# Score products in steps with three double steps per block, and attention blocks of 496 columns, in a two-layer graph kernel

## The chip, the core and the metric

The kernel runs on one core of a Trainium2 chip. The metric is the device time of one launch in microseconds (us). The engines are TensorE (PE; its weight loads are PEld), VectorE (DVE), ScalarE (ACT), GpSimd (POOL) and SyncE (SP, which only issues DMAs here). Every engine works through its own queue in order and waits on semaphores for the others.

## What is computed

Two layers on a graph with 3327 nodes and 128 features. The first is one graph convolution with batch norm; it takes under 3% of the time. The second is an attention over the reshaped features: 128 "batches" d, each with 3327 x 3327 scores of rank 8, to which the adjacency matrix is added twice.

```python
# layer 1, on h = relu(layernorm(x)); n = 3327, d = 128, 8 features per score
q = (x @ Wq.T).reshape(d, n, h)
k = (x @ Wk.T).reshape(d, n, h)
v = (x @ Wv.T).reshape(d, n, h)
a = jnp.einsum('dnh,dmh->dnm', q, k) * scale
a = a + spatial_encoding + edge_encoding      # both are adj
a = jax.nn.softmax(a, axis=2)
out = jnp.einsum('dnm,dmh->dnh', a, v)
return out.reshape(n, h * d) @ Wo.T
```

All is in float32. The scores never go to memory: exp of them is taken on the chip, and numerator and denominator of the softmax come from one product with v and a column of ones.

## The kernel before

**Tiling.** The 128 batches are taken in 32 groups of four. A group goes through seven blocks of columns n (`blocks`, L68: six of 512 and one of 255), and a block through 13 steps. The 3327 rows m lie in 26 chunks c of 128 partitions; a chunk with four batches makes two *pairs* (c, half), each of two batches. So a block has 52 pairs, and a step four of them. `pairs(s)` (L682) says which.

**Two ways for a pair.** A *plain* pair takes its score from PE (`product`, L718, line L725, two matmuls into a PSUM tile of two banks), adds the adjacency on DVE (L818, `scalar_tensor_tensor`, into a third of a tile d), and later ACT takes exp of the whole tile d at once (L856, called `late`, after the first exp of the next step). A *weighted* pair goes past DVE: ACT takes exp of the score straight from PSUM (L828, tile f), and POOL multiplies it by exp of the adjacency terms (L831), which was computed once and lies in DRAM (`wd`). Before, the first 19 chunks are plain (WC = 19): 38 plain and 14 weighted pairs per block. Steps 0 to 11 have three plain pairs and one weighted, step 12 has two of each. A step with two weighted pairs is called a double step below.

**Order in a step.** The order is written by hand (`manual_schedule`), and each engine's queue follows it: score of the weighted pair and its exp; exp of the d of the step before; score and add of plain pair 0; first half of the products with v of the step three before (`second(0)`, L604, eight matmuls; LAG = 3); plain pair 1; plain pair 2, or the second weighted pair; what lies beside (`beside`, L756); the other half of the products with v (`second(1)`). Three PSUM tiles (`psc`) hold scores, two banks (`avs2`) hold the sums over m, there are four tiles d and five tiles f. A sum is ended by `finish` (L609) in four parts, one per step: a copy on DVE (L612), four transposes on PE (L619), three DVE operations (L626 to L629), a DMA.

**Beside it.** Each group loads the q, k, v of the next (`loads`, L153, SP's queue, with 14 casts of k on POOL, L180). Projections for later groups and the last product of earlier ones are spread over the steps: `beside` issues a matmul in step 7 and 10, its evacuation in 8 and 11, and its DMA in 9 and 12. `fetch` (L703) loads adjacency and weights two steps ahead on SP's queue. In group 0 the weights of the blocks 3 to 6 are made on the way (`more_weights`, L734: a load, an exp on ACT, a write); those of the first three are made in the first layer (`weigh_early`, L439).

**The hand-over.** Between the layers, ACT's queue issues the 16 loads of q for group 0 (L580), then sorts part of k (L583), takes the roots of the second norm (L591), and a last exp of weights (L598); the pools of the attention lie where those of the first layer lay.

Of the kernel before, what the change touches and what calls it, by code (L numbers as in the profile page):

```python
# [9 lines left out]
F32 = mybir.dt.float32  # L10
# [8 lines left out]
N = 3327  # L19
D = 128  # L20
# [5 lines left out]
NB = 512  # L26
G = 4
# [4 lines left out]
WC = 19  # L32
CH = 4 * NP // D
NG = D // G
EARLY = 3
# [9 lines left out]
def tile_two_layer_gnn(  # L45
# [23 lines left out]

    const = ctx.enter_context(tc.tile_pool(name="const", bufs=1))  # L70
# [27 lines left out]
    nc.vector.memset(ones, 1.0)  # L98
    eps = const.tile([P, 1], F32, name="eps")
# [29 lines left out]
    def q_loads(q, p0, d):  # L129

        qs = qT[:, bass.ds(d * N, NP)].rearrange("(a h) n -> a h n", h=H)
        return [(q[p0 + i * H : p0 + (i + 1) * H].bitcast(F32), qs[i // 2]) for i in range(4)]
# [153 lines left out]
    with tc.tile_pool(name="l0", bufs=1) as l0, tc.tile_pool(  # L286
        name="l0adj", bufs=3
    ) as ap, tc.tile_pool(name="l0s", bufs=2) as sp, tc.tile_pool(
        name="l0p", bufs=1, space=PSUM
    ) as pp:  # L290
        xs = l0.tile([P, NC, D], F32, name="xs")
        A = l0.tile([P, NC, D], F32, name="A")
        B = l0.tile([P, NC, P], F32, name="B")
# [139 lines left out]
        for y, (n0, w) in enumerate(blocks[:EARLY]):  # L433
            a = ap.tile([P, 7 * NB], F32, name="a")
            a7 = a.rearrange("p (c n) -> p c n", c=7)
            nc.sync.dma_start(a7[:, :, :w], adjr[:, WC:, n0 : n0 + w])
            weights.append((a7, n0, w))

        def weigh_early():  # L439
            a7, n0, w = weights.pop(0)  # L440
            nc.scalar.activation(a7[:, :, :w], a7[:, :, :w], AF.Exp, bias=low, scale=2.0)
            nc.sync.dma_start(
                wd[:, :, n0 : n0 + w].rearrange("c p n -> p c n"), a7[:, :, :w]
            )
# [72 lines left out]
        def residual(i):  # L517
            pt, cs = turned(i, A, acc[i])
            nc.vector.tensor_add(xs[:, cs, :], xs[:, cs, :], pt)
            nc.sync.dma_start(  # L520
                xd.rearrange("(c p) d -> p c d", p=P)[:, cs, :], xs[:, cs, :]
            )
# [20 lines left out]
        ov0 = l0.tile([P, D, H + 1], F32, name="ov0")  # L543
        nc.gpsimd.memset(ov0, 1.0)

        def project_now(j, banks):
            todo = projections(sp, B2[:, j * CH : (j + 1) * CH], j, True, ov0, low_half[:CH, 1:2])
            for p, b in zip(todo, banks):
                drive(p, b)
            for p in todo:  # L550
                drive(p)
                drive(p)
# [23 lines left out]
        for i in range(4, NQ):  # L576
            relu(i)
        for b in range(G):
            for args in q_loads(q, 32 * b, b):
                nc.scalar.dma_start(*args)  # L580
        for x, c in enumerate(range(0, NC, 4)):
            n = min(4, NC - c)
            (nc.scalar.copy if x % 2 else nc.gpsimd.tensor_copy)(  # L583
                k[:, c : c + n, :],
                ks.bitcast(F32).rearrange("g (p c) -> g c p", c=NC)[:, c : c + n, :],
            )
# [8 lines left out]
        for i in range(1, NQ):  # L595
            columns(i, i % 2 == 0)
        keep_columns(0, NQ)
        weigh_early()  # L598


# [8 lines left out]
    def finish(rp, av, d0, n0, w):  # L609

        avs = rp.tile([P, NB], F32, name="avs")
        nc.vector.tensor_copy(avs[:, :w], av[:, :w])  # L612
        yield

        J = 4 if w == NB else 3
        R = w // J
        pt = av.rearrange("p (j q) -> p j q", j=4)
        for j in range(J):
            nc.tensor.transpose(  # L619
                pt[:R, j, :], avs[:, j : j + (R - 1) * J + 1 : J], ident  # L620
            )
        yield
        pv = pt.rearrange("p j (b h) -> p b j h", h=32)
        ri = rp.tile([P, G, 4], F32, name="ri")

        nc.vector.tensor_scalar(ri[:R, :, :J], pv[:R, :, :J, H], 1e-30, None, ALU.max)  # L626
        nc.vector.reciprocal(ri[:R, :, :J], ri[:R, :, :J])  # L627
        o = rp.tile([P, G, 4, H], F32, name="oq")
        nc.vector.tensor_tensor(  # L629
            o[:R, :, :J, :],  # L630
            pv[:R, :, :J, :H],
            ri[:R, :, :J].unsqueeze(3).to_broadcast([R, G, J, H]),
            ALU.mult,
        )
        yield
        nc.sync.dma_start(
            attb[bass.ds(d0, G), n0 : n0 + w, :].rearrange(
                "b (p j) h -> p b (j h)", j=J
            ),
            o[:R, :, :J, :].rearrange("p b j h -> p b (j h)"),  # L640
        )
# [4 lines left out]

    with tc.tile_pool(name="zero", bufs=1) as zp:
        z = zp.tile([P, H], F32, name="zeros")
        nc.gpsimd.memset(z, 0.0)
        nc.gpsimd.dma_start(att[T:, :], z)  # L650

    def attention():


        with tc.tile_pool(name="adj", bufs=4) as ap, tc.tile_pool(
            name="adw", bufs=3
        ) as wp, tc.tile_pool(name="exd", bufs=4) as ep, tc.tile_pool(
            name="exf", bufs=5
        ) as fp, tc.tile_pool(
            name="res", bufs=2  # L660
        ) as rp, tc.tile_pool(name="wk", bufs=2) as wk, tc.tile_pool(
            name="wk1", bufs=1
        ) as wk1, tc.tile_pool(name="psc", bufs=3, space=PSUM) as psc, tc.tile_pool(
# [7 lines left out]
            ov = wk1.tile([P, D, H + 1], F32, name="ov")  # L671
            nc.gpsimd.memset(ov, 1.0)
            if True:
                steps = [
                    (i, y, s)
                    for i in range(NG) for y in range(len(blocks)) for s in range(SU)
# [5 lines left out]
                def pairs(s):  # L682


                    last = s == SU - 1
                    plain = [(j // 2, j % 2) for j in range(3 * s, 3 * s + 3 - last)]
                    rest = [(WC + s // 2, 1 - s % 2)]
                    return plain, rest + ([(NC - 1, 0)] if last else [])
# [3 lines left out]
                for x, (i, y, s) in enumerate(steps):  # L692
                    n0, w = blocks[y]
                    for c, _ in pairs(s)[0]:
                        if (0, i, y, c // 2) not in have:
                            have[0, i, y, c // 2] = None
                            wanted.append((x, 0, i, y, c // 2))
                    c = pairs(s)[1][0][0]
                    if (1, i, y, c) not in have:
                        have[1, i, y, c] = None  # L700
                        wanted.append((x, 1, i, y, c))

                def fetch(x):  # L703
                    while wanted and wanted[0][0] <= x:
                        _, kind, i, y, c = wanted.pop(0)
                        n0, w = blocks[y]
# [11 lines left out]
                def product(i, y, c, half):  # L718
                    q, k, _ = sets[i % 2]
                    n0, w = blocks[y]  # L720
# [10 lines left out]
                waiting, ending, pending = [], [], []  # L731
                late = None

                def more_weights(i, y, s):  # L734

                    k, phase = s // 3, s % 3
                    if i or y + 1 >= len(blocks) or y + 1 < EARLY or k > 3:
                        return
                    n0, w = blocks[y + 1]
# [16 lines left out]
                def beside(i, y, s):  # L756


                    for j in [1, 2] if i == 0 else [i + 2] if i + 2 < NG else []:
                        if (y, s) != (0 if i else 3 * (j - 1), 3):  # L760
                            continue
# [3 lines left out]
                    if s in (8, 11) and extra:  # L765
                        drive(extra[0])
                    if s in (9, 12) and extra:
                        drive(extra.pop(0))
                    if s in (7, 10) and extra:
                        drive(extra[0], avs2[(i * len(blocks) + y + 1) % 2])  # L770
# [3 lines left out]
                extra = []  # L774

                def second(part):

                    (i, y, s), es = waiting[0]
                    n0, w = blocks[y]
                    av = avs2[(i * len(blocks) + y) % 2]  # L780
# [8 lines left out]
                    if part:  # L789
                        waiting.pop(0)  # L790
                        if s == SU - 1:
                            ending.append(finish(rp, av, at(i), n0, w))
# [5 lines left out]

                for x, (i, y, s) in enumerate(steps):
                    n0, w = blocks[y]  # L800
                    fetch(x + PRE)
                    k = x - i * SU * len(blocks) - FROM[i]
# [4 lines left out]
                    while pending and (total - len(pending)) * (SU * len(blocks) - FROM[i] - 4) <= k * total:  # L807
                        pending.pop(0)()
                    more_weights(i, y, s)
                    due = len(waiting) == LAG  # L810
# [14 lines left out]
                    def weighted(c, half):  # L825
                        f = fp.tile([P, 2, NB], F32, name="f")
                        p = product(i, y, c, half)
# [10 lines left out]
                    weighted(*rest[0])  # L838
# [3 lines left out]
                    if due:  # L842
                        second(0)
                    step()
                    add(1, product(i, y, *plain[1]))
                    if len(rest) > 1:
                        weighted(*rest[1])
                    else:
                        add(2, product(i, y, *plain[2]))
                    beside(i, y, s)  # L850
                    if due:
                        second(1)
# [6 lines left out]
                late()  # L859
                while waiting:  # L860
                    second(0)
                    step()
                    second(1)
# [7 lines left out]
    def attention_shifted():  # L871

        with tc.tile_pool(name="shq", bufs=1) as shp, tc.tile_pool(
# [11 lines left out]
            with tc.For_i(0, D, G) as d0:  # L885
# [8 lines left out]
                for y, (n0, w) in enumerate(blocks):  # L894
# [169 lines left out]
```

## Time and profile before

| | us |
|---|---|
| median of 3 runs | 10513.71 (10511.46 to 10516.91) |
| the profiled execution | 10527.91, of it the span of instructions 10526.1 |
| first exp of a weighted pair | 291.66 after the span's start |
| end of the last exp | 10504.8 |
| PE / DVE / ACT / POOL busy | 94% / 92% / 95% / 71% |
| DMA engines | 56.3% of the time of 16 engines on SP's and ACT's queue |

In the profile a row names line, engine, operation, output and inputs and the shape; then come the busy time, the mean duration of one in ns, the idle time before such instructions and what ended it. In a timeline a row is start, duration, instruction, and in brackets idle time before it and its releaser. Consecutive instructions overlap a little, so what one costs on a full engine is read from start to start. A matmul's end in the profile is modelled.

### The profile page before, as it was taken

What the parts mean: (1) busy time and instruction counts of PE and PEld (TensorE: products, weight loads), DVE (VectorE), ACT (ScalarE), POOL (GpSimd) and SP (SyncE); (2) the same over time, 40 slices, a digit from 0 to 9 for tenths busy, and PEclk for the clock granted to TensorE, in tenths of its full rate; (3) what the DMA queues carried; (4) which work ended last, traced back from release to release, by engine and by line L of the source; (5) the groups of instructions that cost most, each with busy time, mean ns of one, the idle gap of its engine ahead of it and who ended that gap; (6) DMA issues with size and microseconds to landing.
All of it is one profiled execution on the core that took longest, in us unless ns stands there. A gap on an engine that the chain in (4) does not pass through costs nothing. (4 is left out here: it accounts for less than half of the span.)

```text
span 10526.1 us, 186778 instructions
## 1 busy us (share of the span) xinstructions
PE 9922.7 (94%) x72399; PEld 2813.8 (27%) x72399; DVE 9714.9 (92%) x9949; ACT 9948.5 (95%) x6200; POOL 7497.1 (71%) x3868
## 2 busy tenths in 40 slices
PE   7889999999999999999999999999999999999999
PEld 3222222222222222222222222222222222222222
DVE  5789999999999999999999999999999999999998
ACT  4889999999999999999999999999999999999998
POOL 0667777777777777777777777777777777777776
PEclk8899999999999999999999999999999999999999
DMA  7655555555555555555555555555555555555554
GB/s 241 192 168 163 157 168 165 163 162 160 162 166 165 164 162 157 161 170 163 160 162 157 165 170 165 160 158 163 164 169 163 162 163 158 165 165 167 156 152 128
DMA packets 1115761, 1731.67 MB, mean 165 GB/s; under 512 B 198350, under 2 KB 441932, under 8 KB 1107180
## 3 DMA queue, kind: packets, MB, share of 16 engines
q1 hardware_dynamic: 1110478, 1713.99, 56.3%
q8 instruction: 568, 9.31, 0.4%
q10 hardware_dynamic: 4350, 5.64, 0.2%
q14 instruction: 333, 2.73, 0.1%
q0 software_dynamic: 32, 0.00, 0.0%
HBM read 1618.76 MB, written 100.53 MB: 163 GB/s over the span
## 5 line engine op out<-in xcount | busy, mean ns | idle before, releaser
L818 DVE SCALAR_TENSOR_TENSOR d<-at,s 128x1024 f32<-128x1024 f32 x8512 | 9204.3, 1138 | 642.7 <-PE s L725 406.2
L831 POOL TENSOR_TENSOR f<-f,wt 128x1024 f32<-128x1024 f32 (+1 forms) x3136 | 6983.8, 2235 | 2619.1 <-ACT f L828 2572.0
L856 ACT ACTIVATE d<-d 128x3072 f32<-128x3072 f32 (+1 forms) x2912 | 7372.9, 2532 | 73.4 <-DVE d L818 70.5
L604 PE MATMUL av<-d,v 128*9 128x512 f32 x34048 | 5528.5, 569 | 0.1
L725 PE MATMUL s<-q,k 32*128 32x512 f32 x23296 | 4280.7, 482 | 505.7 <-DVE d L818 218.0
L725 PEld LDWEIGHTS s<-q,k 32*128 32x128 f32 x23296 | 1773.9, 182 | 5829.2 <-DVE d L818 3312.2
L828 ACT ACTIVATE f<-s 128x1024 f32<-128x1024 f32 (+1 forms) x3136 | 3014.8, 970 | 313.8 <-PE s L725 252.3
L604 PE MATMUL av<-f,v 128*9 128x512 f32 x12544 | 2864.0, 571 | 0.0
L604 PEld LDWEIGHTS av<-d,v 128*9 128x9 f32 x34048 | 630.7, 88 | 1381.6 <-issue 1265.4
L604 PEld LDWEIGHTS av<-f,v 128*9 128x9 f32 x12544 | 310.6, 88 | 52.9 <-issue 41.0
L180 POOL CAST k<-ks 128x256 fp32r<-128x256 f32 x434 | 284.2, 655 | 0.0
L416 PE MATMUL acc<-a,A 128*128 128x512 f32 (+1 forms) x364 | 151.3, 568 | 24.0 <-ACT A L350 23.3
L619 PEld LDWEIGHTS av<-ident,avs 128*128 128x128 f32 (+1 forms) x864 | 121.1, 208 | 179.9 <-issue 178.8
L226 POOL TENSOR_TENSOR o<-pf,o 104x512 fp32r<-104x512 f32 x124 | 160.4, 1293 | 9.9
L619 PE MATMUL av<-ident,avs 128*128 128x128 f32 (+1 forms) x864 | 163.8, 311 | 0.6 <-DVE avs L612 0.6
L225 POOL CAST o<-pf 104x512 fp32r<-104x512 f32 x124 | 75.8, 611 | 115.3 <-DVE pf L224 59.8
L612 DVE COPY avs<-av 128x512 f32<-128x512 f32 (+1 forms) x224 | 144.2, 644 | 2.8 <-PE av L604 2.8
L423 DVE TENSOR_REDUCE amax<-a 128x1 f32<-128x3327 f32 x26 | 93.7, 3610 | 37.7 <-DMA a<-in_adj 37.7
L416 PEld LDWEIGHTS acc<-a,A 128*128 128x128 f32 x364 | 68.8, 192 | 108.8 <-issue 84.4
L420 ACT ACTIVATE junk<-a 128x3327 bf16<-128x3327 f32 x26 | 77.4, 2977 | 6.6 <-DMA a<-in_adj 6.5
L389 POOL TENSOR_TENSOR sq<-wk 128x512 f32<-128x512 f32 x2 | 2.1, 1040 | 102.3 <-PE aside L390 102.3
L629 DVE TENSOR_TENSOR oq<-av,ri 128x128 f32<-128x128 f32 (+1 forms) x224 | 64.1, 286 | 7.7
(120 smaller groups left out, 952.0 us busy)
## 6 DMA issues: line engine op xcount, KB each, us to landing
at<-in_adjT SPq DMA_DIRECT2D x1728, 512.0 KB
wt<-wd SPq DMA_DIRECT2D x1344, 256.0 KB
at<-in_adjT SPq DMA_DIRECT2D x288, 255.0 KB
ks<-kT SPq DMA_DIRECT2D x496, 104.0 KB
q<-qT SPq DMA_DIRECT2D x496, 104.0 KB
at<-in_adjT SPq DMA_DIRECT2D x192, 256.0 KB
a<-in_adj SPq DMA_DIRECT2D x26, 1663.5 KB
wt<-wd SPq DMA_DIRECT2D x224, 127.5 KB
```

The costliest lines, as they stand in the source:

```text
L180: nc.gpsimd.tensor_copy(k[:, c : c + n, half * 64 : half * 64 + 64], ks.bitcast(F32).rearrange("g (p c) -> g c p", c=NC)[:, c : c + n, :],)
L226: nc.gpsimd.tensor_tensor(o[:CH, 1], f[:CH], o[:CH, 0].bitcast(F32), ALU.subtract)
L416: nc.tensor.matmul(acc[i][:, :w], A[:, c, :], a[:, n0 : n0 + w], start=(c == 0), stop=(c == NC - 1),)
L423: nc.vector.tensor_reduce(amax[:, c : c + 1], a[:, :N], AX.X, ALU.max, apply_absolute_value=True)
L604: nc.tensor.matmul(av[32 * b : 32 * b + H + 1, :w], tiles[2][:, b, c, :], e, start=first, stop=last,)
L612: nc.vector.tensor_copy(avs[:, :w], av[:, :w])
L619: nc.tensor.transpose(pt[:R, j, :], avs[:, j : j + (R - 1) * J + 1 : J], ident)
L725: nc.tensor.matmul(p[:, x, :we], k[rs, c, :], q[rs, n0 : n0 + we], start=True, stop=True,)
L818: nc.vector.scalar_tensor_tensor(d[:, j, :, :w], have[0, i, y, c // 2][:, c % 2, :w] .unsqueeze(1).to_broadcast([P, 2, w]), SAFE / 2, p[:, ...
L828: nc.scalar.activation(f[:, :, :w], p[:, :, :w], AF.Exp, scale=2.0)
L831: nc.gpsimd.tensor_tensor(f[:, :, :w], f[:, :, :w], have[1, i, y, c][:, :w].unsqueeze(1).to_broadcast([P, 2, w]), ALU.mult,)
L856: nc.scalar.activation(flat, flat, AF.Exp, scale=2.0)
```

## The change

Four things change.

- `pairs` becomes a table (`kinds`): steps 1, 6 and 10 have two weighted pairs. WC goes from 19 to 18, so a block has 36 plain and 16 weighted pairs.
- `beside` is cut in two. `begin` issues the matmul of a projection, or of an output's product, in a double step, behind the score of the second weighted pair; `go_on` evacuates in the same step and stores in the next one.
- In the step behind a double step the score of the next step's weighted pair is issued before `second(1)` (`first`, `coming`).
- The attention's blocks are 496 wide (`qblocks`: six of 496 and one of 351); the first layer keeps 512.

With it the hand-over changes: only the first 512 columns of q are loaded early, the rest in the first eight steps of group 0 (`others`); the sort of k comes last; early weights are made for 512 columns alone, and `more_weights` runs in six blocks of group 0; `xd` is written at once; the tiles `ov` and `zeros` are set at the start; the pools are laid out in another order.

```diff
-WC = 19
+WC = 18
+QB = 496
-EARLY = 3
+DOUBLE = (1, 6, 10)
...
-        for b in range(G):
-            for args in q_loads(q, 32 * b, b):
+        for b in range(G):
+            for args in q_loads(q, 32 * b, b, 0, NB):
                 nc.scalar.dma_start(*args)
...
+        nc.sync.dma_start(xd.rearrange("(c p) d -> p c d", p=P), xs)
         keep_columns(0, NQ)
-        weigh_early()
+        for x, c in enumerate(range(0, NC, 4)):
+            n = min(4, NC - c)
+            (nc.scalar.copy if x % 2 else nc.gpsimd.tensor_copy)(
...
+                kinds = []
+                for s in range(SU):
+                    j, k = (sum(len(x[i]) for x in kinds) for i in range(2))
+                    n = 2 if s in DOUBLE else 1
+                    kinds.append((
+                        [(x // 2, x % 2) for x in range(j, j + 4 - n)],
+                        [(WC + x // 2, 1 - x % 2) for x in range(k, k + n)],
+                    ))
...
-                    if i or y + 1 >= len(blocks) or y + 1 < EARLY or k > 3:
+                    if i or y + 1 >= len(qblocks) or k > 3:
...
+                def begin(i, y, s):
+                    if extra:
+                        begun.append(extra.pop(0))
+                        drive(begun[0], avs2[(i * len(qblocks) + y + (s > LAG)) % 2])
+
+                def go_on(i, y, s):
+                    if begun and s in DOUBLE:
+                        drive(begun[0])
+                    elif begun:
+                        drive(begun.pop(0))
                     for j in [1, 2] if i == 0 else [i + 2] if i + 2 < NG else []:
-                        if (y, s) != (0 if i else 3 * (j - 1), 3):
+                        if (y, s) != (2 * (j - 1) if i == 0 else 0, 3):
...
-                    if s in (8, 11) and extra:
-                        drive(extra[0])
-                    if s in (9, 12) and extra:
-                        drive(extra.pop(0))
-                    if s in (7, 10) and extra:
-                        drive(extra[0], avs2[(i * len(blocks) + y + 1) % 2])
...
+                    for args in others[:2]:
+                        nc.sync.dma_start(*args)
+                    del others[:2]
...
-                    weighted(*rest[0])
+                    if coming is None:
+                        coming = first(x)
+                    weighted(rest[0][0], coming)
+                    coming = None
                     if late is not None:
                         late()
                     add(0, product(i, y, *plain[0]))
-                    if due:
-                        second(0)
+                    second(0)
                     step()
                     add(1, product(i, y, *plain[1]))
                     if len(rest) > 1:
-                        weighted(*rest[1])
+                        weighted(rest[1][0], product(i, y, *rest[1]))
+                        begin(i, y, s)
                     else:
                         add(2, product(i, y, *plain[2]))
-                    beside(i, y, s)
-                    if due:
-                        second(1)
+                    if s - 1 in DOUBLE:
+                        coming = first(x + 1)
+                    second(1)
+                    go_on(i, y, s)
```

## The prediction

> **What bounds the kernel now.** I read the page first, then the groups by form, the windows, the ACT timeline, the waits.
>
> ```profile
> PE 9922.7 (94%) x72399; PEld 2813.8 (27%) x72399; DVE 9714.9 (92%) x9949; ACT 9948.5 (95%) x6200; POOL 7497.1 (71%) x3868
> ```
>
> Three engines are above 90%, so no share names the bound; the step has to be read. The groups by form give the prices:
>
> ```profile
> L818 DVE SCALAR_TENSOR_TENSOR d<-at,s 128x1024 f32<-128x1024 f32 x7296 | 8417.5, 1213 | 474.6 <-PE s L725 270.4 <-issue 98.4 <-ACT d L856 23.7
> L831 POOL TENSOR_TENSOR f<-f,wt 128x1024 f32<-128x1024 f32 x2688 | 6412.7, 2394 | 2343.2 <-ACT f L828 2303.0 <-DMA q<-qT 19.8 <-DMA wt<-wd 14.6
> L856 ACT ACTIVATE d<-d 128x3072 f32<-128x3072 f32 x2304 | 6398.3, 2777 | 60.4 <-DVE d L818 59.1 <-ACT f L828 0.2
> ...
> L828 ACT ACTIVATE f<-s 128x1024 f32<-128x1024 f32 x2688 | 2753.2, 1032 | 239.1 <-PE s L725 211.8 <-POOL k L180 12.6 <-POOL f L831 7.2
> ```
>
> The waits say the same in other words (engine and line, what it waited for, us in total, times, longest):
>
> ```profile
> POOL f L831 <- ACT f L828: 2572.0, 2228, 4.1
> ...
> DVE d L818 <- PE s L725: 406.2, 785, 2.3
> ACT f L828 <- PE s L725: 252.3, 380, 7.6
> ```
>
> POOL waits for ACT; ACT waits little, and mostly for PE's scores. The windows of the preamble, of group 0 and of the other 31 groups:
>
> ```profile
> 0.00:291.00 291.00, 197.45 (x513) 94.31 (x513) 148.79 (x259) 130.09 (x136) 28.26 (x48) 0.86 0.72 237
> 291.00:669.00 378.00, 328.25 (x2190) 84.82 (x2190) 306.34 (x303) 320.67 (x205) 241.54 (x130) 0.91 0.62 179
> 669.00:10505.00 9836.00, 9390.30 (x69665) 2629.25 (x69661) 9257.26 (x9381) 9497.75 (x5860) 7227.12 (x3691) 0.99 0.56 162
> ```
>
> 9836 / 31 = 317.3 us per group. The ACT timeline around a block's double step, and four steps later:
>
> ```profile
> 5033.73 1.04 ACT L828 ACTIVATE f<-s 128x1024 f32<-128x1024 f32 x1
> 5034.63 2.79 ACT L856 ACTIVATE d<-d 128x3072 f32<-128x3072 f32 x1
> 5037.29 1.96 ACT L828 ACTIVATE f<-s 128x1024 f32<-128x1024 f32 x2
> 5039.10 1.95 ACT L856 ACTIVATE d<-d 128x2048 f32<-128x2048 f32 x1
> 5040.90 1.07 ACT L828 ACTIVATE f<-s 128x1024 f32<-128x1024 f32 x1
> ...
> 5058.74 1.06 ACT L828 ACTIVATE f<-s 128x1024 f32<-128x1024 f32 x1
> 5060.15 2.77 ACT L856 ACTIVATE d<-d 128x3072 f32<-128x3072 f32 x1 [0.34 <-DVE d L818]
> ```
>
> Start to start with nothing waited for, f takes 0.90 us, d 2.66, the short d 1.80: a step is 3.56, and ACT sets it. DVE needs 3 x 1.13 = 3.39 (back-to-back starts of L818), so it regains only 0.17 a step. What a block's end puts on DVE (avs 0.68; ri, oq 0.71) and four transposes on PE use that up, and in step 6 ACT waits for DVE, as the last line shows.
>
> **ACT's floor and the excess.** Steps are counted 0 to 12 in a block, blocks 0 to 6 in a group. Old wide block: 14 x 0.90 + 12 x 2.66 + 1.80 = 46.3. The narrow one shows f 0.49 and d 1.37 where they touch: 14 x 0.49 + 12 x 1.37 + 0.96 = 24.3. Group: 6 x 46.3 + 24.3 = 302.1. So 15.2 of 317.3 us is excess. By the starts of L828, blocks 0 to 6 of a usual group take 48.1, 48.3, 48.3, 47.3, 48.3, 46.9 and 29.1. Block 5 has nothing beside it, and its 0.6 is the block end. Two projections in a block cost 1.4 more (steps 7, 10 and the next step 0, about 0.5 each), the last output product 1.4. The narrow block has 4.8: its steps are 2.03, not 1.86, because of a loop DVE, PE, DVE (score 0.38, av products 0.55, score, L818 0.68, three score buffers).
>
> **What the Trainium skill says.** "ScalarE: Activation LUTs", What ACT_TABLE_LOAD costs: an activation takes 186 ns + 0.833 ns per element, and neighbours overlap by about 93. That gives 1039 and 2745 ns; the rows have 1032 and 2777: it agrees, and splitting work differently among activations costs only some 0.09 each. "GPSIMD Engine Reference", Elementwise side by side: a two-input operation is about 2.6 cycles per element; the rows, 2394 at 1024 and 1284 at 510, give 2.16 ns per element, which is that at the 1.2 GHz of its specifications. The same page's Specifications say that GpSimd shares its SBUF interface with VectorE and collides with DVE instructions that have two SBUF inputs. L818 has one (the other is PSUM), and it stays at 1.21 us whether POOL runs or not (5066 to 5080): a busier POOL should not slow it.
>
> **The change, part by part.**
>
> 1. ACT. Elements stay. Per element 0.833 ns: at 496, f 0.875, d 2.58, short d 1.75; at 351, 0.65, 1.85, 1.26. New wide block 16 x 0.875 + 10 x 2.58 + 3 x 1.75 = 45.05; narrow 10.4 + 18.5 + 3.8 = 32.7. Group 6 x 45.05 + 32.7 = 303.0. The floor rises by 0.9: no gain there; all must come from the excess.
>
> 2. DVE loses 2 of 38 L818 per block, 2.3 us in a wide one: 36 x 1.10 = 39.6 + block end 1.4 against 45.05. It is no longer the second bound on average, but three score buffers let it run ahead by less than two us, so relief counts only where it falls.
>
> 3. POOL: 16 x 2.33 = 37.2 per wide block, 27.2 narrow, 14 casts of k 9.7, four projection pairs 7.6: 268 of some 312 us. Around a double step it runs 3 us behind, and the f is read three steps (10 us) later: hidden. If the cover were gone, a double step would grow by 1.2 (two f, 4.65, against 3.46).
>
> 4. A double step (one with two weighted pairs). In the old block ends (block 5 to 6 and 4 to 5) the short step and the following ones show 2.71 and 3.56, ACT's floor. The second f waits for the long d, its buffer comes free behind it, then p1 and p2 of the next step: L818 ends 0.5 us before ACT wants the d. So DVE leaves each double step with a lead of 0.5 (its d is ready 0.5 us before ACT comes to it), whatever it had before. The product brought forward spares nothing that waited there; it pushes the second half of the av products behind it by 0.4, and these free the fifth f buffer for the same exp. I cost it at 0; the margin is about 0.2 us.
>
> 5. Block end. Copy in step 3, transposes in 4, ri and oq in 5: gross 0.60, 0.49 and 0.73 on DVE's lead. Old lead in step 2 is 0.85 (0.5 behind the old double step, then 0.17 a step); new, one step after the double step 1, 0.5. The stall grows from 0.6 to about 0.9 (0.5 to 1.3): 6 x 0.9 = 5.4.
>
> 6. Projections and outputs lie in double steps, where DVE idles 1.9 us (two gaps of 1.0 and 0.9 around 5037): matmul 0.95 on PE, evacuation 0.7. In steps 6 and 10: 0. In step 1, before a block end: 0.3, three times. The last output product (sixteen matmuls, about 2.3 us on PE) still delays the next f by 1.0. Sum 2.0 (0.5 to 5) against 9 now.
>
> 7. Narrow block of 351: loop 0.88 + 0.06 + 0.36 + 0.71 + 0.47 = 2.48 (interpolated between the forms) against ACT's 2.50: no longer PE's. Excess 4.8 to 2.0 for the block end: 34.7.
>
> Group: 270.3 + 5.4 + 2.0 + 34.7 = 312.4, saving 4.9; 31 groups 152.
>
> 8. Preamble. ACT issues 16 loads of q from 233.8 to 270.3 before it takes the roots at 273.5; then comes an exp of 3.3 and a wait of 6.9 for its write, so that the first f is at 291.7. With short q loads the next gate is k, landed at 264.0, its sort 3.9 and a product: 268. Minus 24 (10 to 35). The 16 remaining loads go by SP at 0.3 to 0.5 each, two per step: nothing.
>
> 9. Group 0 makes weights in six blocks instead of four. Block 2 there costs 54.0 against 48.3, so 2 x 5.7 more, with the shared saving: plus 7 (0 to 40).
>
> Sum: 152 + 24 - 7 = 169 less. The profiled execution was 10527.9 (span 10526.1), 14 above the median of the runs, so it becomes about 10359, and the median 10513.7 - 169, near 10345.
>
> **The rivals.**
>
> A, as above: 10345, own range 10250 to 10440. Chance 0.54.
>
> B, the stalls go nearly everywhere: 305 per group (2 over the floor), 31 x 12.3 = 381 + 17: 10115. For it: DVE gains 16 us a group. Against: block ends come two steps behind a double step, where the lead is reset. 0.19.
>
> C, slower: PE's order behind a double step. f of the step after next needs both its product and the f buffer that the av products now queued behind that product free; the projection's matmul (0.95) is in the same queue, and behind it wait all av products, the next scores and so DVE. Price: step 0 now takes 3.09 instead of 2.71 where a projection lies before it, 0.38; 21 double steps a group: 8.0, group 320.4, 31 x 3.1 = 96 more, less 17: 10595. It decides from 0.24 us per double step. Against it: block 5's clean 2.71. 0.19.
>
> D, gains and losses cancel, within 0.2% (21 us, about what a measurement of this kernel tells from none): a group near 317. 0.08.
>
> That the change does less than it says is in A already: in part 4 the product brought forward buys nothing.
>
> **Numbers.** Faster by over 0.2%: A, B and a little less: 0.73; within 0.08; slower 0.19. Range: from the faster part of B, 10070, to D and the start of C, 10545; outside lie most of C and the ends.
>
> **What would show it.** L818 x8064 in place of 8512, L828 x3584. Right if ACT's starts show 3.46 in single steps and f, f, short d touching in steps 1, 6 and 10; if waits of ACT for PE's scores shrink below 252 us; if the first f comes near 268. Step 6 should still show ACT waiting for DVE, about 0.9. Wrong if f in steps 3, 8 or 12 waits for PE (C), or if POOL f shows few waits for ACT and av products wait for POOL (POOL paces).

## The result, and the profile after

| | before | after |
|---|---|---|
| median | 10515.86 (6 runs) | 10469.31 (6 runs, 10463.21 to 10474.28) |
| ratio to before | | 0.9955 (0.9944 to 0.9965) |
| span of the profiled execution | 10526.1 | 10470.4 |
| first f / group 0 / groups 1 to 31 | 291.7 / 377.1 / 9836.1 | 259.9 / 415.5 / 9773.3 |

The change gained 46.5 us where 169 were forecast. The last row is read from the starts of the weighted exps (f), and it says where: the hand-over between the layers gained 31.8 us (forecast 24), group 0 lost 38.4 (forecast 7), and the other 31 groups gained 62.8, or 2.0 each (forecast 152, or 4.9 each). The two profiled executions lie 56 us apart, more than the medians, because that of the kernel before was 12 us above its median. Taken from the medians, the gain of the 31 groups is nearer to 1.7 each.

The page after, busy time and then the groups by form. The columns are those of the rows shown for the kernel before:

```profile
PE 9899.3 (95%) x72399; PEld 2827.8 (27%) x72399; DVE 9326.7 (89%) x9501; ACT 10000.4 (96%) x6655; POOL 8421.2 (80%) x4315
```

```profile
L837 DVE SCALAR_TENSOR_TENSOR d<-at,s 128x992 f32<-128x992 f32 x6912 | 7814.4, 1183 | 813.5 <-PE s L727 596.6 <-ACT d L879 106.1 <-issue 20.6
L849 POOL TENSOR_TENSOR f<-f,wt 128x992 f32<-128x992 f32 x3072 | 7068.3, 2319 | 1575.9 <-ACT f L846 1539.4 <-DMA wt<-wd 9.5 <-issue 8.6
L879 ACT ACTIVATE d<-d 128x2976 f32<-128x2976 f32 x1920 | 5167.2, 2691 | 79.2 <-DVE d L837 74.7 <-ACT f L846 1.7
...
L846 ACT ACTIVATE f<-s 128x992 f32<-128x992 f32 x3072 | 3006.1, 1000 | 122.8 <-PE s L727 66.1 <-PE av L610 17.7 <-POOL f L849 9.4
```

DVE lost 388 us of busy time and idles more, most of it for PE's scores; ACT is at 96%. The waits of ACT have moved rather than gone:

```profile
ACT d L879 <- DVE d L837: 97.0, 246, 0.7
ACT f L846 <- PE s L727: 85.4, 225, 3.9
ACT t L755 <- DMA t<-in_adjT: 44.5, 10, 10.5
```

Waits for PE's scores fell from 252 to 85 us, as they should. Waits of the long exp for DVE rose from 70.5 to 97.0, though DVE has less to do. The third line is new in this size (14.5 before): the exp that makes weights waits for its load. A fourth wait stands further down the same list, and the kernel before does not have it: the exp of a weighted pair (f) waits for products with v, which free its buffer.

```profile
ACT f L846 <- PE av L610: 40.4, 82, 2.7
```

The windows of the hand-over, of group 0, and of the other groups (engine columns as before, then the granted PE clock, DMA share and GB/s):

```profile
0.00:260.00 260.00, 199.02 (x513) 93.87 (x513) 148.97 (x259) 124.58 (x136) 28.94 (x49) 0.91 0.68 228
260.00:675.00 415.00, 352.35 (x2182) 87.08 (x2182) 293.40 (x288) 330.59 (x226) 269.94 (x142) 0.84 0.68 196
675.00:10449.00 9774.00, 9340.67 (x69669) 2641.32 (x69669) 8881.65 (x8947) 9545.23 (x6294) 8122.34 (x4124) 1.00 0.61 163
```

In group 0 ACT is busy for 331 of 415 us, and PE's clock is at 0.84, against 0.91 in the kernel before and 1.00 later.

The ACT timeline of steps 1 to 6 of block 4 in a usual group (start, duration, instruction, and what idle time before it was waited for):

```profile
5279.49 0.99 ACT L846 ACTIVATE f<-s 128x992 f32<-128x992 f32 x1
5280.37 2.70 ACT L879 ACTIVATE d<-d 128x2976 f32<-128x2976 f32 x1
5282.94 1.89 ACT L846 ACTIVATE f<-s 128x992 f32<-128x992 f32 x2
5284.70 1.88 ACT L879 ACTIVATE d<-d 128x1984 f32<-128x1984 f32 x1
5286.46 1.01 ACT L846 ACTIVATE f<-s 128x992 f32<-128x992 f32 x1
...
5289.93 1.00 ACT L846 ACTIVATE f<-s 128x992 f32<-128x992 f32 x1
5290.91 2.69 ACT L879 ACTIVATE d<-d 128x2976 f32<-128x2976 f32 x1
5293.79 1.00 ACT L846 ACTIVATE f<-s 128x992 f32<-128x992 f32 x1 [0.19 <-PE s L727]
5294.73 2.69 ACT L879 ACTIVATE d<-d 128x2976 f32<-128x2976 f32 x1
5297.32 0.98 ACT L846 ACTIVATE f<-s 128x992 f32<-128x992 f32 x1
5298.99 2.69 ACT L879 ACTIVATE d<-d 128x2976 f32<-128x2976 f32 x1 [0.69 <-DVE d L837]
```

The double step 1 touches (f, f, short d), as forecast. Step 4 (from 5289.93) takes 3.86 instead of 3.45, and in step 6 the long exp waits 0.69 for DVE. The DVE timeline of the same stretch has the block end in it:

```profile
5284.54 3.50 DVE L837 SCALAR_TENSOR_TENSOR d<-at,s 128x992 f32<-128x992 f32 x3 [0.59 <-PE s L727]
5287.96 0.67 DVE L618 COPY avs<-av 128x496 f32<-128x496 f32 x1
5288.54 3.37 DVE L837 SCALAR_TENSOR_TENSOR d<-at,s 128x992 f32<-128x992 f32 x3
5292.35 3.38 DVE L837 SCALAR_TENSOR_TENSOR d<-at,s 128x992 f32<-128x992 f32 x3 [0.43 <-PE s L727]
5295.65 0.17 DVE L632 TENSOR_SCALAR ri<-av 124x16 f32<-124x16 f32 x1
5295.85 0.26 DVE L633 RECIPROCAL ri<-ri 124x16 f32<-124x16 f32 x1
5296.14 0.29 DVE L635 TENSOR_TENSOR oq<-av,ri 124x128 f32<-124x128 f32 x1
```

DVE idles behind the double step (0.59: the scores come late), then gets the copy, then waits for scores that stand behind the four transposes in PE's queue (0.43), then has the divisions. So its idle time does not lie where the block end needs it.

### The profile page after: what moved, and what is told of

It is laid out like the page before. It is cut to its first block, busy times and chain, and to the rows that moved or that the text cites. A ratio compares the mean times of both kernels' runs of the same rounds, so it can differ in the third digit from the quotient of the medians.

```text
span 10470.4 us, 188308 instructions
## 1 busy us (share of the span) xinstructions
PE 9899.3 (95%) x72399; PEld 2827.8 (27%) x72399; DVE 9326.7 (89%) x9501; ACT 10000.4 (96%) x6655; POOL 8421.2 (80%) x4315
## 3 DMA queue, kind: packets, MB, share of 16 engines
q14 instruction: 345, 2.83, 0.1%
## 4 chain that ended last, share of the span: by engine, by line
PE 36%; POOL 19%; DVE 18%; ACT 13%; issue 10%; DMA 1%; SPq 0%; ACTq 0%; DVEq 0%; POOLq 0%
PE av L610 18%; POOL f L849 18%; DVE d L837 16%; PE s L727 15%; ACT f L846 9%; ACT d L879 4%; PE av L625 1%; DVE avs L618 1%; POOL o L237 1%; PE av L276 1%; DMA wt<-wd 1%; DVE ri L633 0%; DMA t<-in_adjT 0%; PE av L207 0%; POOL o L236 0%
## 5 line engine op out<-in xcount | busy, mean ns | idle before, releaser
L837 DVE SCALAR_TENSOR_TENSOR d<-at,s 128x992 f32<-128x992 f32 x8064 | 8781.5, 1140 | 963.8 <-PE s L727 686.5
L849 POOL TENSOR_TENSOR f<-f,wt 128x992 f32<-128x992 f32 (+1 forms) x3584 | 7926.0, 2229 | 1786.2 <-ACT f L846 1749.5
L879 ACT ACTIVATE d<-d 128x2976 f32<-128x2976 f32 (+1 forms) x2912 | 7010.3, 2407 | 101.5 <-DVE d L837 97.0
L610 PE MATMUL av<-d,v 128*9 128x496 f32 x32256 | 5094.2, 569 | 0.8 <-ACT d L879 0.8
L727 PE MATMUL s<-q,k 32*128 32x496 f32 x23296 | 4260.4, 477 | 505.0 <-DVE d L837 259.2
L846 ACT ACTIVATE f<-s 128x992 f32<-128x992 f32 (+1 forms) x3584 | 3382.9, 966 | 166.8 <-PE s L727 85.4
L610 PE MATMUL av<-f,v 128*9 128x496 f32 x14336 | 2862.6, 568 | 0.0
L610 PEld LDWEIGHTS av<-d,v 128*9 128x9 f32 x32256 | 583.9, 88 | 1306.7 <-issue 1291.6
L610 PEld LDWEIGHTS av<-f,v 128*9 128x9 f32 x14336 | 316.8, 88 | 153.9 <-issue 148.0
L625 PEld LDWEIGHTS av<-ident,avs 128*124 128x124 f32 (+1 forms) x864 | 122.4, 208 | 178.8 <-issue 177.5
L625 PE MATMUL av<-ident,avs 128*124 128x128 f32 (+1 forms) x864 | 165.0, 312 | 0.6 <-DVE avs L618 0.6
L618 DVE COPY avs<-av 128x496 f32<-128x496 f32 (+1 forms) x224 | 144.8, 646 | 3.5 <-PE av L610 3.5
```

The source lines that it names most:

```text
L610: nc.tensor.matmul(av[32 * b : 32 * b + H + 1, :w], tiles[2][:, b, c, :], e, start=first, stop=last,)
L625: nc.tensor.transpose(pt[:R, j, :], avs[:, j : j + (R - 1) * J + 1 : J], ident)
L727: nc.tensor.matmul(p[:, x, :we], k[rs, c, :], q[rs, n0 : n0 + we], start=True, stop=True,)
L837: nc.vector.scalar_tensor_tensor(d[:, j, :, :w], have[0, i, y, c // 2][:, c % 2, :w] .unsqueeze(1).to_broadcast([P, 2, w]), SAFE / 2, p[:, ...
L846: nc.scalar.activation(f[:, :, :w], p[:, :, :w], AF.Exp, scale=2.0)
L849: nc.gpsimd.tensor_tensor(f[:, :, :w], f[:, :, :w], have[1, i, y, c][:, :w].unsqueeze(1).to_broadcast([P, 2, w]), ALU.mult,)
```

## The experiments

"Group" below is the mean of groups 1 to 30, taken from the starts of f in each run's trace: 317.4 before, 315.2 after. Each comes from one execution; that of the kernel before was 12 us slow, which is up to 0.4 in its group. Ratios are to the kernel before.

**Parts of the change.** First the width, undone in the change and made alone in the kernel before.

```diff
-QB = 496
+QB = 512
```

> The change with blocks of 512 and 255 again, the rest as it is. Theory 1 (ACT sets the step; what is left above its floor is the block end, the steps behind double steps and the narrow block): wide blocks 46.4 + 1.1, narrow 24.4 + 4: 315.6 to 316.2 per group against 315.2, so 10475 to 10510 us against 10469. If the width were what gained the 2 us per group (rival), the group returns to 317 and the run to 10520 or more.

Measured: 10533.67 us, ratio 1.0020 (1.0012 to 1.0027), group 317.4. The rival held. With 512 columns the double steps and the moved projections are worth nothing: a group takes what it took before, and the run by its median is even 19 us longer.

```diff
+QB = 496
...
+    qblocks = [(n0, min(QB, N - n0)) for n0 in range(0, N, QB)]
...
-                    n0, w = blocks[y]
+                    n0, w = qblocks[y]
```

> The kernel before with attention blocks of 496 and 351, nothing else. Theory 2 (the width alone gained what the 31 groups gained, through a narrow block whose steps ACT again sets): a group falls from 317.4 to 315.3 to 316.3, the run to 10450 to 10480 us. Rival (the width needs the double steps to gain): 10505 us or more.

Measured: 10435.70 us, ratio 0.9922 (0.9905 to 0.9938), group 314.6. One number alone gains more than the whole change, and more than was expected of it. The narrow block takes 34.8 us: 2.2 over its floor of 32.6, where the narrow block of 255 columns was 4.8 over its own. The six wide ones keep their excess (10.0 in place of 10.4). So in the change, the rest costs 0.6 us a group on top of what the width gains.

```diff
-                    if s - 1 in DOUBLE:
-                        coming = first(x + 1)
```

> The change without the product brought forward in the step behind a double step. Theory 1: the product brought forward puts off the next scores and costs DVE 0.2 to 0.35 us of its lead two steps later, so without it a block end stalls a little less: 10400 to 10470 us. Rival (PE's order, the product spares what its author moved it for): the exp behind the step behind waits up to 0.4 in 21 places per group: up to 10720 us.

Measured: 10449.67 us, ratio 0.9942 (0.9926 to 0.9959), group 315.1. The product brought forward is worth nothing in the usual groups. It takes from one step and gives to another: without it step 4 takes 3.5 to 3.8 instead of 3.86, and a step behind a double step with a projection 3.0 instead of 2.86. The 20 us of the run lie in group 0 (396.5 against 415.5). That group moves by almost as much between runs that leave its weights alone (401.4 in the run without block ends, 402.5 in the run with half of POOL's work), so they are not put down to the product.

**The block end.** Its arithmetic left out, in both kernels:

```diff
-        avs = rp.tile([P, NB], F32, name="avs")
-        nc.vector.tensor_copy(avs[:, :w], av[:, :w])
...
-            nc.tensor.transpose(
-                pt[:R, j, :], avs[:, j : j + (R - 1) * J + 1 : J], ident
-            )
...
-        o = rp.tile([P, G, 4, H], F32, name="oq")
...
+        o = oconst
```

> The changed kernel without the arithmetic of the block end: copy, transposes, reciprocal and division are left out, and a tile of ones is stored in their place (the attention's output is left out with them). Theory 1 (the block end meets a DVE that a double step has just left with a lead of 0.5 us): the 1.1 us of stall per wide block and about 1.9 in the narrow one go, a group to 306 to 307.5, the run to 10195 to 10235 us. Rival (the excess is PE's order or POOL around double steps): a group stays above 312, the run above 10370 us.

> The kernel before with the same part left out. Theory 1: there the block end comes four steps behind the double step and costs only 0.6 per wide block and some 2.4 in the narrow one, so a group falls from 317.4 to 311 to 312.5, the run to 10325 to 10370 us, less than in the changed kernel. Rival (a block end costs the same in both): the falls are equal.

Measured: the changed kernel 10237.26 us, ratio 0.9740 (0.9724 to 0.9757), group 308.2; the kernel before 10367.07, ratio 0.9861 (0.9844 to 0.9877), group 312.6. So the same block end costs 7.0 us a group after the change and 4.8 before it; by the medians it costs the whole run 232 us after and 150 before, which sets the two further apart. Block 5, which has nothing beside it, shows it purest: 46.17 to 45.19 after, 46.89 to 46.30 before. So the rival, an equal price in both kernels, fails. But the changed kernel's group was expected at 306 to 307.5: without any block end it still has 5.2 us above ACT's floor of 303.0. Steps 4 to 6 of block 4 without the block end, 3.45 from f to f (step 6 is the double step, and its second f begins at 5190.44):

```profile
5180.09 1.00 ACT L829 ACTIVATE f<-s 128x992 f32<-128x992 f32 x1
5180.96 2.70 ACT L862 ACTIVATE d<-d 128x2976 f32<-128x2976 f32 x1
5183.54 1.01 ACT L829 ACTIVATE f<-s 128x992 f32<-128x992 f32 x1
5184.42 2.70 ACT L862 ACTIVATE d<-d 128x2976 f32<-128x2976 f32 x1
5186.99 1.02 ACT L829 ACTIVATE f<-s 128x992 f32<-128x992 f32 x1
5187.87 2.72 ACT L862 ACTIVATE d<-d 128x2976 f32<-128x2976 f32 x1
5190.44 1.91 ACT L829 ACTIVATE f<-s 128x992 f32<-128x992 f32 x2
```

Then the double steps were moved, the number of them and all work the same.

```diff
-DOUBLE = (1, 6, 10)
+DOUBLE = (4, 8, 12)
...
-                    if extra:
+                    if extra and s > 6:
...
-                    if s - 1 in DOUBLE:
+                    if (s - 1) % SU in DOUBLE:
```

The second edit keeps the projections to steps 8 and 12; with it the loads for group 1 start two steps later in group 0.

> Double steps at 4, 8 and 12 instead of 1, 6 and 10, so that one lies in the block end (steps 3 to 5); projections and outputs in 8 and 12 alone. Same work. Theory 1: the block end's stall of 1.1 per wide block falls to about 0.3, a group to 310 or 311, the run to 10310 to 10350 us. Rival (POOL, 80% busy, paces around double steps): their number and POOL's work stay, so 10455 to 10485 us.

Measured: 10321.21 us, ratio 0.9822 (0.9806 to 0.9839), group 311.0, as the theory had it. Projections move with the double steps here; block 5, which has none, falls from 46.17 to 45.58 and shows what the place alone is worth (0.59; six such blocks would make 3.5 of the group's 4.2). ACT around the double step 4, which begins with the f at 5207.54:

```profile
5204.96 2.69 ACT L879 ACTIVATE d<-d 128x2976 f32<-128x2976 f32 x1
5207.54 1.00 ACT L846 ACTIVATE f<-s 128x992 f32<-128x992 f32 x1
5208.42 2.69 ACT L879 ACTIVATE d<-d 128x2976 f32<-128x2976 f32 x1
5211.02 1.87 ACT L846 ACTIVATE f<-s 128x992 f32<-128x992 f32 x2
5212.77 1.86 ACT L879 ACTIVATE d<-d 128x1984 f32<-128x1984 f32 x1
5214.74 1.00 ACT L846 ACTIVATE f<-s 128x992 f32<-128x992 f32 x1
5215.88 2.69 ACT L879 ACTIVATE d<-d 128x2976 f32<-128x2976 f32 x1
```

The whole block end now costs ACT some 0.5 us (0.3 was expected): 0.2 at 5214.74, where a d of 1.75 ends, and 0.26 ahead of the next d.

```diff
-DOUBLE = (1, 6, 10)
+DOUBLE = (0, 5, 9)
...
-                    if s - 1 in DOUBLE:
+                    if (s - 1) % SU in DOUBLE:
```

> Double steps at 0, 5 and 9. Theory 1 in numbers: the copy of step 3 and the transposes of step 4 meet a lead of 0.35 and stall ACT by about 0.5, the double step 5 takes up the rest; so 0.5 per wide block, between 1.1 (1, 6, 10) and 0.3 (4, 8, 12): a group 311.5 to 312.5, the run 10350 to 10390 us. Rival (4, 8, 12 gained by something else than the block end's place): no order by the distance from the block end.

Measured: 10442.81 us, ratio 0.9927 (0.9911 to 0.9944), group 314.5. The number missed. Block 5 lies between the other two (45.89, against 46.17 and 45.58), so the order by place holds, but with 0.8 of excess and not 0.5: step 4 gives 0.46 as worked out, and the step behind step 5 another 0.2. What I had not counted is a projection in step 5: its matmul goes to the bank that the block end is read from in that step, so it waits for the divisions on DVE, the scores behind it come late, and such a step takes up to 5.3 us instead of 4.4:

```profile
5137.17 1.10 PE L207 MATMUL av<-wq,hj 128*104 128x512 f32 x2 [1.03 <-DVE oq L635]
```

**POOL.**

```diff
-                            f[:, :, :w], f[:, :, :w],
-                            have[1, i, y, c][:, :w].unsqueeze(1).to_broadcast([P, 2, w]),
+                            f[:, :1, :w], f[:, :1, :w],
+                            have[1, i, y, c][:, :w].unsqueeze(1).to_broadcast([P, 1, w]),
```

> The changed kernel with POOL's product of the weighted exps done for one of the two batches of a pair (the other is left unweighted). Theory 1 (POOL is hidden): no more than 0.5 us per group, 10450 to 10475 us. Rival (POOL, 80% busy, paces around double steps): a group falls by over 2, the run below 10410 us.

Measured: 10459.45 us, ratio 0.9948 (0.9932 to 0.9965), group 315.2.

POOL's row of the groups by form in this run:

```profile
L849 POOL TENSOR_TENSOR f<-f,wt 128x496 f32<-128x496 f32 x3072 | 3826.9, 1252 | 4745.0 <-ACT f L846 4720.0 <-DMA wt<-wd 9.0 <-issue 8.7
```

POOL's work in this row nearly halves, its idle time triples, and a group stays as it was to 0.1 us. POOL hides behind ACT, double steps or not, although the chain of waits of the changed kernel put 18% of the span on it.

**Group 0.**

```diff
-                    if i or y + 1 >= len(qblocks) or k > 3:
+                    if i or y + 1 >= len(qblocks) or y + 1 < 3 or k > 3:
...
+                            n0 = n0 if y > 2 else 0
```

> The changed kernel without the weights of the second and third block being made in group 0 (these blocks read the first block's weights in every group, so the weights used there are others). Theory: the two blocks added to that work cost 22 to 32 us, group 0 falls from 401 to 415 to 380 to 392, the run to 10437 to 10450 us. Rival (group 0 is slow for its start and its loads): less than 10 us.

Measured: 10441.15 us, ratio 0.9928 (0.9911 to 0.9944); group 0 385.6, the others 315.2. Without the two added blocks of weights group 0 is 30 us shorter and the run 28. They cannot be given all of that: in the other runs that make weights for six blocks and leave their loads alone, group 0 lies anywhere from 395.3 to 410.8, so their share is 10 to 30 us of the 38.

```diff
+                    if phase == 0 and k:
+                        c = WC + 2 * k - 2
+                        nc.sync.dma_start(
+                            wd[c - WC : c - WC + 2, :, n0 : n0 + w].rearrange("c p n -> p c n"),
+                            have["w"][:, :, :w],
+                        )
...
-                    elif phase == 1:
+                    elif phase == 2:
```

> The change with the exp of the weights made in group 0 two steps after their load instead of one, and their write a step later still. Theory: ACT waits in order for these loads (44.5 us in ten waits in group 0) and everything behind it stops; group 0 falls from 415 to 360 to 375, the run by 40 to 55 to 10415 to 10430 us; other groups stay at 315.2. Rival (DMA or POOL limits group 0 whatever the order): no more than 10 us.

Measured: 10444.89 us, ratio 0.9938 (0.9921 to 0.9954); group 0 396.7, the others 314.9. Group 0 was expected at 360 to 375: it lost 19 us, and the run 24, where 40 to 55 were expected. The waits of the weights' exp in group 0 fell from 44.5 us to 12.4, but those of f for PE's scores rose from 18.8 to 38.6. With the trace's tile view of the weights' tile, first the changed kernel (idle time of ACT until a load landed), then this one:

```profile
  DMA t<-in_adjT: 44.5, 10
```

```profile
  DMA t<-in_adjT: 8.0, 5
  DMA ks<-kT: 4.4, 1
```

**Versions.** Double steps at 4, 8, 12 with the later weights' exp, first without the product brought forward, then with it.

> Double steps at 4, 8 and 12, no product brought forward, and the weights' exp in group 0 two steps behind their load. Theory: a group 310 to 311, group 0 some 20 less than with the double steps alone: 10270 to 10310 us.

Measured: 10333.24 us, ratio 0.9829 (0.9813 to 0.9846), group 312.3, group 0 366.2. The run and the group missed (10270 to 10310, 310 to 311 expected): with these double steps the product brought forward is worth 1.3 us a group. A step behind a double step with a projection takes 3.03 without it and 2.86 with it. Behind step 4 the block end still takes the difference back (step 6 takes 3.47 without it and 3.73 with it); behind steps 8 and 12 nothing does.

> Double steps at 4, 8 and 12 with the product brought forward kept, and the weights' exp in group 0 two steps behind their load. Theory: a group 311.0 as with these double steps alone, group 0 at 365 to 380: 10285 to 10310 us, faster than both kernels and than every run so far.

Measured: 10299.57 us, ratio 0.9794 (0.9778 to 0.9811), group 311.0, group 0 374.3. It is the fastest of the kernels that compute everything: 2.1% below the kernel before, 1.6% below the change.

Its windows of group 0 and of the other groups, columns as above:

```profile
260.00:634.00 374.00, 326.31 (x2190) 84.34 (x2190) 291.79 (x289) 330.65 (x227) 268.67 (x141) 0.91 0.76 218
634.00:10276.00 9642.00, 9397.89 (x69657) 2692.18 (x69653) 8844.66 (x8947) 9505.67 (x6294) 8126.09 (x4125) 1.00 0.61 165
```

ACT is busy for 9506 of 9642 us in its usual groups; before the change it was 9498 of 9836.

## Why the prediction was wrong

What held is the frame: ACT sets the step, its floor rises a little, and all gain is taken from the excess above it. The direction held too, but for one of its two reasons only. Of the 4.9 us a group some 2.6 were to come from the wider narrow block, and some 2.3 from the double steps and what was moved into them. The width gained 2.8 by itself; the double steps lost 0.6 beside it, and with 512 columns they gained nothing. That the kernel got faster at all it owes to the width. The result lies outside the range of the way that was held likeliest (10250 to 10440).

By the traces the sum was off by 113 us: 89 in groups 1 to 31 and 31 in group 0, while the hand-over gave 8 more than forecast. The groups in terms (us per group; "before" and "measured" are from the mean blocks of the traces, with and without the block end):

| term | before | forecast | measured |
|---|---|---|---|
| ACT's floor (part 1, worked out) | 302.1 | 303.0 | 303.0 |
| block end in six wide blocks (part 5) | 3.3 | 5.4 | 5.6 |
| all else in the wide blocks (parts 4 and 6) | 7.1 | 2.0 | 3.3 |
| block end in the narrow block (part 7) | 1.5 | 2.0 | 1.4 |
| all else in the narrow block (parts 4 and 7) | 3.3 | 0 | 2.0 |
| group | 317.3 | 312.4 | 315.3 |

- **Part 5 held, in mechanism and size.** The long exp of step 2 starts 0.53 us after its last sum on DVE ends (median of the wide blocks), 0.5 was forecast; the lead is down to 0.09 in steps 3, 4 and 5. The block end costs block 5 1.0 us, 0.9 was forecast. Over all blocks it costs 7.0 a group, 7.4 were forecast.
- **Parts 4 and 7 are the first step that failed.** The narrow block was given no excess but its block end. Without block ends it still takes 34.7 us, over a floor of 32.7. That 34.7 was also forecast, with the block end in it, is chance. Of the 2.0 us, 0.7 is a matter of counting: read from f to f, the narrow block holds the last long exp of the wide block before it (2.58 in place of 1.85), and block 0 of the next group is spared as much. The rest lies behind its double steps. These three steps take 2.51, 2.25 and 2.25 where f and short d touch at 1.9. Part 4 put the wait for the f buffer that the products with v free at nothing, with a margin of 0.2 us. In the narrow block there is no such margin, as the run without block ends shows in a step behind a double step and the f after it:

```profile
5276.58 1.41 ACT L862 ACTIVATE d<-d 128x1404 f32<-128x1404 f32 x1
5278.20 0.76 ACT L829 ACTIVATE f<-s 128x702 f32<-128x702 f32 x1 [0.21 <-PE av L612]
```

  Without the product brought forward these waits are gone from the list, but those of f for its scores rise from 85 to 168 us, so the loss is not the product's alone.
- **Part 6** was too low: 3.3 us are left in the wide blocks beside the block end, 4.0 with the 0.7 that block 0 is spared. A projection in step 6 or 10 costs 0.2 and not 0 (2.83 to 2.86 in the next step instead of 2.62), the output product 0.6 instead of 1.0, and 0.14 is lost in each wide block even with nothing beside it, mostly behind the double steps. "Against 9 now" did not fit part 6's own numbers either: 15.2 less 3.6 and 4.8 is 6.8. (The blocks listed there add up to 316.3; the mean of block 0 is 48.8 and not 48.1.)
- **Part 9 is the other step that failed**: 38.4 us for 7, within the range given but at its end. I took a block with weights at 5.7 us from block 2 of the kernel before, where one exp waited for its load. Three more blocks of that trace make weights on the way, and they take 60.8, 63.2 and 63.0 us, 13 to 16 more than in a usual group. At the mean of all four, 12.5, two more blocks are 25 us and not 11. In the changed kernel the exp waits up to 10.5 us in ACT's queue, and what stands behind it there waits too.
- **Part 8** forecast 24 and got 31.8: the first f is at 259.9 instead of 268, as k lands some 10 us earlier when q's loads are short. Part 3 held (no change with half of POOL's work), and part 2 in that relief of DVE counts only where it falls. Of part 4, the product brought forward is worth nothing in this place, as forecast (315.1 without it).
- **The rivals.** B did not come about: the relief of DVE by 16 us a group lies in double steps, where it idles for PE's scores. C came about in part: the steps behind double steps lose 3.5 us a group together (2.3 in the wide blocks, most of it where a projection lies, and 1.2 in the narrow one), 0.17 per double step where C put 0.38. The waits for DVE in step 6 that the forecast named as a sign are there (0.69, about 0.9 forecast).

Against the kernel before with 496 columns the terms show what the double steps did. Block 5 is taken here as the measure of what every wide block pays for block end and double steps. What lies beside falls from 6.4 to 2.2 us a group, a gain of 4.2. The six wide blocks pay 3.1 more (1.1 each in place of 0.6), the narrow one 1.2 more, and the floor is 0.7 higher.

What stays open is the rest of group 0. Of its 415 us, 315 are those of any group and about 24 the weights' exps themselves. Waits for loads are 44.5, but taking most of them away gained only 19 to 24 (21 with the double steps at 4, 8 and 12), and the rest went into waits for PE. PE's granted clock is a possible reason. The Trainium skill, "TensorE: Matmul & The Clock Gate", What's actually happening, says that PE's clock is halved after some 3.4 us without work and comes back after as long a busy time. The trace agrees with it in kind: the eight products of L610 take 1.84 us at 278.5 and 1.02 at 399.4, and the clock is 0.84 over the group. Over all runs the length of group 0 goes with this clock: 366 to 368 us at 0.93, 374 to 377 at 0.91, 385 to 397 at 0.87 to 0.89, 401 to 411 at 0.85 to 0.87, 415 at 0.84. The waits for the weights' loads do not order the runs so (49 us where the group takes 396.5, 17 where it takes 410.8). But PE may lose its clock because the group stalls, or the group may stall for the clock: no run here changed the clock alone, so this is argued, not shown.

## What to carry to other kernels

When one engine sets the pace, relief for the second is worth something only where the second makes the first wait; find those steps by name, and put the relief into them, not next to them. A change that gains in one row of a table (projections, 4.2 us) should be priced on the rows beside it as well: here the step that takes the load off also resets how far ahead DVE is, and the next burst meets it unready. When such a step is made shorter, in a narrower block, look again at every wait that was put at nothing: its margin shrinks with it. A price should be taken from all places that the profile has, not from the first one. And run each part of a change alone: one number, the block width, was worth more than the change.

## What was not expected of the hardware

A block of 351 columns runs at ACT's pace and one of 255 does not: in the kernel before, most single steps take 2.03 us with 255 columns, against 1.86 on ACT, and 2.48 to 2.50 with 351, against 2.50. A last block that is a little wider, for the same number of columns in all, saved 2.6 us a group there. That the loop of a score buffer through PE and DVE has a part that does not shrink with the width would explain it; no run isolates that part.

The steps are very regular. In block 5 of the changed kernel the steps in which nothing is lost differ by 0.01 to 0.02 us over 30 groups; those of the block end and those behind double steps differ by 0.3 to 0.6. So losses of 0.2 us per step can be read from the mean or median over the groups of one trace.
